# Attention in blocks of 64 for two heads at a time, with row maxima and inverse sums spread through memory, in an attention and mixture-of-experts layer

## The chip, the cores and the metric

The kernel runs on one core of one Trainium2 chip. A core has five engines that run side by side and wait for each other through semaphores: PE (TensorE, matrix products), DVE (VectorE), ACT (ScalarE), POOL (GpSimd) and SP (SyncE, which here only issues transfers). [...] The metric is the time of one execution on the device in microseconds (us), as the median of several runs.

## The reference, cut to what matters

The input x has 8 batches of 512 tokens with 256 features. One normalised copy feeds two branches, and both are added to x.

```python
xn = layernorm(x)                       # 8 x 512 x 256
# attention: 16 heads of 16 features, each query sees keys within 64 positions
q, k, v = split(xn @ Wqkv + bqkv)
scores = q @ k.T * 16 ** -0.5           # per head, 512 x 512
scores = where(abs(i - j) <= 64, scores, finfo.min)
attn = softmax(scores)                  # over keys
a = (attn @ v) @ Wout + bout
# experts: 8 experts, 256 -> 1024 -> 256, the best 2 of each token
f = sum over top 2 of gate * (relu(xn @ w1[e] + b1[e]) @ w2[e] + b2[e])
out = x + a + f
```

All of the matrix products below are in 32-bit floats. One such product appears in the profile as two matmul records.

## The kernel before

**Stages.** The first part (the loop over `UNITS` and `route`) normalises, transposes xn to features by tokens (`xnT`), computes router scores, picks two experts for each token and works out for each of up to 71 expert tiles of 128 slots which tokens it takes. From there on a single loop over `ROUNDS` = 69 rounds of two steps interleaves attention with the expert tiles. Engine order is written out by hand: every engine executes its instructions in the order of the program text, and so does SP with its transfers.

**Expert tiles.** `expert_pieces` gives a list of pieces with a cost: `first_layer(i, 0)` with the transposes of the next tile (9), `second_layer(i - 1)` (16), `first_layer(i, 1)` (8). After the attention work of a step, pieces are popped until the cost done so far reaches the step's share. `first_layer` makes 16 products `h`, and ACT applies bias and ReLU (L808); `turn` transposes gathered tokens (`px`) and DVE copies them (L792); `second_layer` makes 8 products `y` with 256 columns, DVE scales them (L823) and POOL issues a scatter that adds them to the output in memory (L824). `load_1` and `load_2` have SP fetch 1 MB of weights each into buffers that the tile before the last must have left. POOL also issues the gathers of tokens and gates (L715, L725).

**Attention.** The 16 heads of a batch are eight strips of 32 features, a strip holding two heads, `j` = 0 and 1. A *pair* `p` is half a batch: four strips (`a` = 0 to 3, 32 partitions each); there are `PAIRS` = 16. For each pair:

- `dense` (two pairs ahead) makes q and k of the pair. Both exist twice, once for each head of a strip, with the other head's 16 rows zeroed (`at`, `qat`). One row of the zeroed half, `ROW[j]`, is put to use: k holds 1 there, and q will hold minus the row maximum there.
- `maxima(p, n)`, n = 0 to 7, called from `search` one step after another: a block of 128 queries against the 192 or 256 keys of its band (`sc`, four products, 32 rows deep, in two row groups of PE), and then DVE takes with a mask the maximum of each query (L955), negated, into `nms`.
- `put_maxima`: PE transposes `nms` (`nt`), DVE adds it into the free row of q (L977). So the next product gives scores with the maximum already subtracted.
- `weigh(p, n)`: a block of 128 keys against 192 or 256 queries (`st`, four products), ACT takes the exponential from PSUM (L999), POOL zeroes what is outside the band with four selects (L1009, L1014).
- `values(p, n)`: the weights times v (`av`, four products that write 32 partitions each). It runs two units at a time in the first step of the next round. v (`vA`, made by `vals`) has a column of ones per head, so that row `DH * (1 - j)` of the result is the sum of the weights. ACT copies `av` to SBUF (L1045), once for each of the two heads.
- The sums go to memory (`put_sums`), come back 128 partitions wide (`gather_sums`), are inverted (L1067), go to memory (`put_inverses`) and are spread over the 16 rows of each head (`spread_inverses`, eight transfers into `bc`); `scale` multiplies and adds the two heads (L1087, L1088). The table `divide` says in which step of the next pair each runs. For the last pair `scale_at_once` spreads the sums with a product (`den`) instead.
- `project` multiplies with Wout once per batch (`po`), and POOL issues one transfer that adds the batch to the output (L1119).

In step `m` = 2 * round + part the order is: `weigh` of pair p, `search` of unit m + 1 (which belongs to the next pair), on even steps `values` of the two units of the round before, then `dense`, `vals`, `project`, then one step of `divide`, then expert pieces, then on some steps `put_maxima`. On PE a step is therefore st, sc, (av), others, expert products. `weigh` and `search` of one step use opposite strips (`ah` differs), so their products lie in different row groups of PE.

**Buffers that matter.** `st` has one PSUM buffer (`ps_t`), `sc` two (`ps_c`), `av` one (`ps_a`); h, px, y, qk, v, po and nt share three (`ps_m`). The weights `p` have three SBUF buffers.

Of the kernel before, what the change touches and what calls it, by code (L numbers as in the profile page):

```python
# [22 lines left out]
def kernel(  # L23
# [24 lines left out]

    A, G = 4, 4
# [20 lines left out]
    qk_pool = ctx.enter_context(tc.tile_pool(name="qk_pool", bufs=3))  # L70
    o_pool = ctx.enter_context(tc.tile_pool(name="o_pool", bufs=4))
# [64 lines left out]
    raw = p_pool.tile([P, KC, 2 * D], F32, tag="p", name="raw")  # L136
# [46 lines left out]
    for k in range(KC):  # L183
# [21 lines left out]
    mask = const.tile([P, 2 * P], F32, tag="mask", name="mask")  # L205
    nc.gpsimd.memset(mask, 0.0)
    nc.gpsimd.affine_select(
        out=mask, in_=mask, pattern=[[1, 2 * P]], compare_op=ALU.is_ge, fill=NEG,
        base=0, channel_multiplier=-1,
    )  # L210
    nc.gpsimd.affine_select(
        out=mask, in_=mask, pattern=[[-1, 2 * P]], compare_op=ALU.is_ge, fill=NEG,
        base=2 * HALF, channel_multiplier=1,
    )
# [3 lines left out]
    vA, nms = [], []  # L218
    bc = wk1.tile([P, 2, N], F32, tag="bc", name="bc")

    def clear():

        for i in range(2):
            t = wk1.tile([P, NT, NH // 2, 2, 32], F32, tag=f"vA{i}", name=f"vA{i}")
            nc.gpsimd.memset(t.rearrange("p t h j c -> p (t h j c)"), 0.0)
            nc.gpsimd.memset(t[:, :, :, 0, DH : DH + 1], 1.0)
            nc.gpsimd.memset(t[:, :, :, 1, 0:1], 1.0)
            vA.append(t)

        for n in range(2):  # L230
            t = wk1.tile([P, NT, A, 32], F32, tag=f"nm{n}", name=f"nm{n}")
            nc.gpsimd.memset(t.rearrange("p t a r -> p (t a r)"), 0.0)
            nms.append(t)

        nc.gpsimd.memset(bc.rearrange("p j q -> p (j q)"), 0.0)


    ROW = [DH, 0]
# [4 lines left out]
    hot = const.tile([P, 2], F32, tag="hot", name="hot")  # L243
    bqk = const.tile([P, 3, 2], F32, tag="bqk", name="bqk")

    kb_ = const.tile([P, 2, 2], F32, tag="kb", name="kb")
    qb_ = const.tile([P, 2, 2], F32, tag="qb", name="qb")

    def places():
        nc.vector.tensor_scalar(place_i, place_i, 31, None, ALU.bitwise_and)  # L250
        nc.vector.tensor_copy(place, place_i)
        for j, op in enumerate((ALU.is_lt, ALU.is_ge)):
            nc.vector.tensor_scalar(at[:, j : j + 1], place, float(DH), None, op)
            nc.vector.tensor_scalar(hot[:, j : j + 1], place, float(ROW[j]), None, ALU.is_equal)
        nc.vector.tensor_scalar(qat, at, QSCALE, None, ALU.mult)


    choice = const.tile([P, 2, P], F32, tag="choice", name="choice")

    def choices():  # L260
        nc.vector.memset(choice.rearrange("p j m -> p (j m)"), 0.0)
        for j in range(2):
            for a in range(A):
                nc.vector.tensor_copy(
                    choice[32 * a : 32 * a + 32, j, 32 * a : 32 * a + 32],
                    hot[32 * a : 32 * a + 32, j : j + 1].to_broadcast([32, 32]),
                )

    def qk_bias():
        bps = ps_m.tile([P, 512], F32, tag="m", name="bps")  # L270
        transpose(bps[:, 0:6], braw.rearrange("q a r -> q (a r)"), ident[:6, :6])
        nc.scalar.copy(bqk.rearrange("p s i -> p (s i)"), bps[:, 0:6])
        full = [P, 2, 2]
        for to, s, by in ((kb_, 1, at), (qb_, 0, qat)):
            nc.vector.tensor_mul(
                to, bqk[:, s].unsqueeze(2).to_broadcast(full), by.unsqueeze(1).to_broadcast(full)
            )
        nc.vector.tensor_add(kb_, kb_, hot.unsqueeze(1).to_broadcast(full))
# [164 lines left out]
    sel = p_pool.tile([P, 2, TOPK, NA, E], F32, tag="p", name="sel")  # L443
    sel = sel[:, 0]
# [349 lines left out]
    def first_layer(i: int, part: int):  # L794
# [11 lines left out]
        for n in range(HC // 2):  # L806
            c = part * HC // 2 + n
            nc.scalar.activation(  # L808
                s["hT"][:, c, :], ph[:, n, :], AF.Relu, bias=s["tb"][:, c : c + 1]
            )  # L810
# [65 lines left out]
    def reach(t: int):  # L876


        lo, hi = max(0, t * P - HALF), min(N, (t + 1) * P + HALF)
        return lo, hi, lo - (t * P - HALF)  # L880
# [3 lines left out]
    def dense(p: int, s: int, by_act: bool = False, steps=range(KC + 1)):  # L884

        b, i = p // 2, p % 2
        if s == 0 and 0 in steps:
            qk[p] = tuple(
                qk_pool.tile([P, 2, N], F32, tag=n, name=f"{n}_{p}") for n in ("q", "k")
            )  # L890
# [10 lines left out]
        if KC not in steps:  # L901
            return
        for j in range(2):
            to = qk[p][s][:, j, :]
            if s == 1:
                nc.scalar.activation(
                    to, pm, AF.Identity, bias=kb_[:, i, j : j + 1], scale=at[:, j : j + 1]
                )
            elif by_act:
                nc.scalar.activation(  # L910
                    to, pm, AF.Identity, bias=qb_[:, i, j : j + 1], scale=qat[:, j : j + 1]
                )
            else:
                nc.vector.tensor_scalar(
                    to, pm, bqk[:, 0, i : i + 1], qat[:, j : j + 1], ALU.add, ALU.mult
                )

    def vals(b: int, t: int):
        pm = ps_m.tile([P, 512], F32, tag="m", name=f"v_{b}_{t}")
        for k in range(KC):  # L920
            matmul(
                pm[:, 0:D], xnT[b][:, k, ts(t, P)], wv[:, k, :],
                start=(k == 0), stop=(k == KC - 1),
            )

        to = vA[b % 2][:, t].rearrange("p h j c -> p h (j c)").rearrange(
            "p h (u d) -> p h u d", d=DH
        )[:, :, 0:4:3, :]
        nc.scalar.copy(to, pm[:, 0:D].rearrange("p (h j d) -> p h j d", j=2, d=DH))

    first = [(h, j, ah) for h in range(2) for j in range(2) for ah in range(2)]
    second = [(j, h, ah) for j in range(2) for h in range(2) for ah in range(2)]

    def maxima(p: int, n: int):

        half, j, ah = first[n]
        q, k = qk[p]
        sc = []
        for c in range(2):
            sc.append(ps_c.tile([P, 2, 2 * P], F32, tag="c", name=f"sc_{p}_{n}_{c}"))  # L940
        for i in range(2):
            qb = 2 * half + i
            lo, hi, off = reach(qb)
            for c in range(2):
                r = 32 * (2 * ah + c)
                matmul(
                    sc[c][:, i, 0 : hi - lo], q[r : r + 32, j, ts(qb, P)],
                    k[r : r + 32, j, lo:hi], start=True, stop=True,
                )
        for c in range(2):  # L950
            for i in range(2):
                qb = 2 * half + i
                lo, hi, off = reach(qb)
                junk = wk.tile([P, 2 * P], BF16, tag="junk", name=f"jk_{p}_{n}_{c}_{i}")
                nc.vector.tensor_tensor_reduce(  # L955
                    out=junk[:, 0 : hi - lo],
                    in0=sc[c][:, i, 0 : hi - lo],
# [5 lines left out]
                    accum_out=nms[p % 2][:, qb, 2 * ah + c, ROW[j] : ROW[j] + 1],  # L963
                )

    def put_maxima(p: int, half: int):

        pm = ps_m.tile([P, 2 * P], F32, tag="m", name=f"nt_{p}_{half}")
        for i in range(2):
            transpose(  # L970
                pm[:, ts(i, P)],
                nms[p % 2][:, 2 * half + i].rearrange("p a r -> p (a r)"), ident,
            )
        for j in range(2):
            to = qk[p][0][:, j, ts(half, 2 * P)]

            nc.vector.scalar_tensor_tensor(  # L977
                to, pm, at[:, 1 - j : 2 - j], to, ALU.mult, ALU.add
            )
# [3 lines left out]
    def weigh(p: int, n: int):  # L983

        j, half, ah = second[n]
        q, k = qk[p]
        st = ps_t.tile([P, 2, 2, 2 * P], F32, tag="t", name=f"st_{p}_{n}")
        for i in range(2):
            kb = 2 * half + i
            lo, hi, off = reach(kb)  # L990
            for c in range(2):
                r = 32 * (2 * ah + c)
                matmul(
                    st[:, c, i, off : off + hi - lo], k[r : r + 32, j, ts(kb, P)],
                    q[r : r + 32, j, lo:hi], start=True, stop=True,
                )
        w = weights[p, n] = p_pool.tile([P, 2, 2, 2 * P], F32, tag="p", name=f"p_{p}_{n}")
        cut = slice(HALF, 4 * P) if half == 0 else slice(0, 4 * P - HALF)
        nc.scalar.activation(  # L999
            w.rearrange("k c i q -> k c (i q)")[:, :, cut],  # L1000
            st.rearrange("k c i q -> k c (i q)")[:, :, cut],
            AF.Exp,
        )

        for i in range(2):
            lo, hi, off = reach(2 * half + i)
            end = off + hi - lo
            one = w[:, :, i, off:P]
            nc.gpsimd.affine_select(  # L1009
                out=one, in_=one, pattern=[[0, 2], [1, P - off]], compare_op=ALU.is_ge,  # L1010
                fill=0.0, base=off, channel_multiplier=-1,
            )
            two = w[:, :, i, P:end]
            nc.gpsimd.affine_select(  # L1014
                out=two, in_=two, pattern=[[0, 2], [-1, end - P]], compare_op=ALU.is_ge,
                fill=0.0, base=0, channel_multiplier=1,
# [4 lines left out]
    def values(p: int, n: int):  # L1021

        j, half, ah = second[n]
        b, pair = p // 2, p % 2
        if half == 0 and ah == 0:
            av[p, j] = ps_a.tile([P, N], F32, tag="av", name=f"av_{p}_{j}")
        w = weights.pop((p, n))

        for i in range(2):
            kb = 2 * half + i  # L1030
            lo, hi, off = reach(kb)
            for c in range(2):
                a = 2 * ah + c
                matmul(
                    av[p, j][32 * a : 32 * a + 32, lo:hi],
                    vA[b % 2][:, kb, 2 * a + pair, j, :],
# [289 lines left out]
```

## Time and profile before

Three runs took 916.38 us in the median (915.89 to 919.32). The profile is of one execution that took 917.28 us, with a span of 915.2 us; 2.1 us lie around the span. The granted PE clock was 0.987 of full speed over the span.

| What | us | of what |
|---|---|---|
| span of the profiled execution | 915.2 | its time 917.28 |
| ACT bias and ReLU of `hT` | 157.4 | 552 of 0.368 us |
| DVE masked maximum of `sc` | 198.3 | 256 of 0.421 us (256 wide), 256 of 0.354 us (192 wide) |
| ACT exponential | 117.5 | 128 of 0.918 us (896 wide) |
| POOL selects | 285.4 | 384 of 128 x 256, 128 of 128 x 128 |
| DVE add of the maxima into q | 27.8 | 64 of 0.476 us (128 x 256) |
| DVE multiply and add of the division | 29.7 | 15 of 1.257 us, 15 of 0.719 us |
| ACT copy of `av` | 18.7 | 32 of 0.586 us |
| q1, SP's transfers | 57.9% of 16 engines' span | 172.07 MB |
| q0, POOL's transfers | 13.3% of 16 engines' span | 22.33 MB |

Busy time is the sum over an engine's instructions with overlaps counted once. Records of matmuls overlap, so the durations of single ones do not add up to what PE needs for them; the distance from the start of one group to the start of the next does.

### The profile page before, as it was taken

The page shows a single profiled execution, that of the slowest core. Times are in us where ns is not written, and L with a number is a line of the kernel's source. Part 1 is how long each engine was busy: PE and PEld are TensorE (multiplying, and loading weights), DVE is VectorE, ACT ScalarE, POOL GpSimd, SP SyncE. Part 2 cuts the span into 40 slices and gives each one's busy share as a digit, 9 for nine tenths or more (in the row PEclk, how much of TensorE's full clock was granted, in tenths as well). Part 3 has the DMA queues.
Part 4 walks back from the last instruction along what each step waited for, and adds up shares of the span by engine and source line. Part 5 has one row for each costly group of instructions (what it writes and reads, how often), then busy time and mean ns, then how long its engine had stood idle before and what let it go on. Part 6 is the DMA issues. An engine that isn't in the chain of part 4 may idle for free.

```text
span 915.2 us, 20492 instructions
## 1 busy us (share of the span) xinstructions
PE 878.4 (96%) x7264; PEld 704.5 (77%) x7264; DVE 389.5 (43%) x1523; ACT 390.6 (43%) x923; POOL 457.7 (50%) x770
## 2 busy tenths in 40 slices
PE   5878999999999999999999999999999999999896
PEld 2457888788877788887887878777887878888685
DVE  6775533444344434343435343535343434331140
ACT  6652334444543454434443445344534444443231
POOL 4014345555554555464655565555545644664522
PEclk9997999999999999999999999999999999999899
DMA  9954887776675867577767677878777756987763
GB/s 292 315 171 136 242 271 220 222 231 222 199 241 179 215 206 233 172 209 218 221 197 202 200 221 231 211 222 261 219 195 219 235 174 216 250 254 226 195 193 41
DMA packets 154199, 196.26 MB, mean 214 GB/s; under 512 B 26456, under 2 KB 131928, under 8 KB 154096
## 3 DMA queue, kind: packets, MB, share of 16 engines
q1 hardware_dynamic: 133698, 172.07, 57.9%
q0 software_dynamic: 19680, 22.33, 13.3%
q8 instruction: 58, 0.95, 0.4%
q10 hardware_dynamic: 718, 0.54, 0.2%
q14 instruction: 45, 0.37, 0.1%
HBM read 172.71 MB, written 22.18 MB: 213 GB/s over the span
## 4 chain that ended last, share of the span: by engine, by line
PE 91%; DVE 3%; DMA 3%; issue 1%; ACT 1%; POOL 1%; POOLq 0%; DVEq 0%; ACTq 0%
PE h L92 28%; PE y L92 26%; PE st L92 10%; PE av L92 7%; PE qk L92 6%; PE sc L92 4%; PE po L92 4%; PE v L92 3%; PE px L95 2%; DMA x<-in_L_attn_x_dram 1%; DMA out_dram<-yo,dest 1%; PE nt L95 1%; DMA xs<-xd,tok 1%; ACT xn L371 1%; PE xt L95 0%
## 5 line engine op out<-in xcount | busy, mean ns | idle before, releaser
L92 PEld LDWEIGHTS h<-xT,w 128*128 128x128 f32 x2208 | 262.8, 194 | 22.0 <-issue 16.9
L808 ACT ACTIVATE hT<-h,b 128x128 f32<-128x128 f32 x552 | 157.4, 368 | 279.3 <-PE h L92 229.7
L92 PE MATMUL h<-xT,w 128*128 128x128 f32 x2208 | 271.8, 280 | 0.0
L92 PE MATMUL y<-w,hT 128*128 128x256 f32 x1104 | 252.7, 382 | 0.0
L92 PEld LDWEIGHTS y<-w,hT 128*128 128x128 f32 x1104 | 206.0, 190 | 38.7 <-issue 10.4
L824 POOL DMA_INDIRECT out_dram<-yo,dest x69 | 112.1, 1625 | 232.0 <-DVE yo L823 185.5
L955 DVE CUSTOM_DVE_ANT_0 jk<-sc,mask 128x256 bf16<-128x256 f32 (+1 forms) x512 | 170.1, 387 | 117.5 <-PE sc L92 114.2
L999 ACT ACTIVATE p<-st 128x896 f32<-128x896 f32 x128 | 117.5, 918 | 189.9 <-PE sc L92 157.2
L1009 POOL TENSOR_SCALAR_AFFINE_SELECT p<-p 128x256 f32<-128x256 f32 (+1 forms) x256 | 137.3, 563 | 116.2 <-ACT p L999 110.2
L1014 POOL TENSOR_SCALAR_AFFINE_SELECT p<-p 128x256 f32<-128x256 f32 (+1 forms) x256 | 141.2, 582 | 0.0
L92 PE MATMUL sc<-k,q 32*128 32x192 f32 (+1 forms) x1024 | 132.1, 375 | 0.0
L92 PE MATMUL st<-q,k 32*128 32x192 f32 (+1 forms) x1024 | 131.3, 374 | 0.0
L823 DVE SCALAR_TENSOR_TENSOR yo<-y,g,b2g 128x256 f32<-128x256 f32 x69 | 33.4, 484 | 179.7 <-issue 100.0
L92 PEld LDWEIGHTS st<-q,k 32*128 32x128 f32 x1024 | 83.6, 184 | 27.5 <-issue 23.2
L792 DVE COPY xT<-px 128x256 f32<-128x256 f32 x69 | 29.3, 424 | 152.7 <-PE px L95 102.1
L92 PEld LDWEIGHTS sc<-k,q 32*128 32x128 f32 x1024 | 84.1, 185 | 2.2 <-issue 1.8
L715 POOL DMA_INDIRECT xs<-xd,tok x69 | 70.6, 1023 | 24.2 <-issue 10.5
L725 POOL DMA_INDIRECT g<-gd,gate x69 | 65.8, 954 | 21.0 <-issue 20.7
L92 PE MATMUL av<-p,vA 128*32 128x192 f32 (+1 forms) x1024 | 64.7, 360 | 4.3 <-POOL p L1014 4.3
L92 PE MATMUL qk<-xnT,wqk 128*128 128x512 f32 x128 | 62.8, 615 | 0.0
L92 PEld LDWEIGHTS av<-p,vA 128*32 128x32 f32 x1024 | 29.6, 109 | 28.1 <-issue 15.8
L955 DVE DVE_READ_ACCUMULATOR2_ANT nm<- 128x1 f32 x512 | 42.5, 83 | 0.0
(181 smaller groups left out, 584.8 us busy)
## 6 DMA issues: line engine op xcount, KB each, us to landing
w<-in_L_ffn_w_dram SPq DMA_DIRECT2D x120, 1024.0 KB
w<-in_L_ffn_w_dram SPq DMA_DIRECT2D x36, 512.0 KB
b<-in_L_ffn_b_dram SPq DMA_DIRECT2D x69, 128.0 KB
x<-in_L_attn_x_dram SPq DMA_DIRECT2D x8, 512.0 KB
xd<-xn SPq DMA_DIRECT2D x8, 512.0 KB
out_dram<-x SPq DMA_DIRECT2D x8, 512.0 KB
out_dram<-sum POOLq DMA_DIRECT2D x8, 512.0 KB
bc<-d SPq DMA_DIRECT2D x120, 32.0 KB
```

Source lines behind the costliest of these rows:

```text
L92: return pe(nc.tensor.matmul(*args, **kwargs))
L95: return pe(nc.tensor.transpose(*args))
L715: nc.gpsimd.indirect_dma_start(out=tx, out_offset=None, in_=xd, in_offset=bass.IndirectOffsetOnAxis(ap=tok[:, i : i + 1], axis=0),)
L725: nc.gpsimd.indirect_dma_start(out=tg, out_offset=None, in_=gd, in_offset=bass.IndirectOffsetOnAxis(ap=gate[:, i : i + 1], axis=0),)
L792: nc.vector.tensor_copy(s["xT"], px)
L808: nc.scalar.activation(s["hT"][:, c, :], ph[:, n, :], AF.Relu, bias=s["tb"][:, c : c + 1])
L823: nc.vector.scalar_tensor_tensor(yo, py[:, 0:D], s["tg"], b2g, ALU.mult, ALU.add)
L824: nc.gpsimd.indirect_dma_start(out=by_token, out_offset=bass.IndirectOffsetOnAxis(ap=dest[:, i : i + 1], axis=0), in_=yo, in_offset=None, ...
L955: nc.vector.tensor_tensor_reduce(out=junk[:, 0 : hi - lo], in0=sc[c][:, i, 0 : hi - lo], in1=mask[:, off : off + hi - lo], scale=-1.0, sca ...
L999: nc.scalar.activation(w.rearrange("k c i q -> k c (i q)")[:, :, cut], st.rearrange("k c i q -> k c (i q)")[:, :, cut], AF.Exp,)
L1009: nc.gpsimd.affine_select(out=one, in_=one, pattern=[[0, 2], [1, P - off]], compare_op=ALU.is_ge, fill=0.0, base=off, channel_multiplier=-1,)
L1014: nc.gpsimd.affine_select(out=two, in_=two, pattern=[[0, 2], [-1, end - P]], compare_op=ALU.is_ge, fill=0.0, base=0, channel_multiplier=1,)
```

## The change

Blocks are now of `BK` = 64 queries or keys, and one product does both heads of a strip. What is held twice, with the other head zeroed, is the 64-wide block that PE keeps (2 x 64 columns); what streams past is the plain strip. `reach` gives 192 columns (128 at the two ends) instead of 256 and 192. The number of products stays: 512 each of sc, st and av.

```diff
     def reach(t: int):
-        lo, hi = max(0, t * P - HALF), min(N, (t + 1) * P + HALF)
-        return lo, hi, lo - (t * P - HALF)
+        lo, hi = max(0, (t - 1) * BK), min(N, (t + 2) * BK)
+        return lo, hi, lo - (t - 1) * BK
```

`dense` makes q doubled and k plain (k: one ACT operation instead of two); for `weigh` the other way round is needed, and `other_way` makes it: DVE adds the two halves of q, ACT makes k doubled with two operations.

`vals` makes v with the two heads on different halves of the partitions: eight products of 128 columns that write 64 partitions each, instead of two of 256 columns; ACT copies one half, DVE the other.

```diff
+        for n in range(2):
+            for k in range(KC):
+                for j in range(2):
+                    matmul(
+                        pm[ts(j, BK), ts(n, P)], xnT[b][:, k, ts(2 * t + n, BK)],
+                        wv[:, k, :].rearrange("p (h j d) -> p h j d", j=2, d=DH)[:, :, j, :],
+                        start=(k == 0), stop=(k == KC - 1), skip_group_check=True,
+                    )
```

`maxima` keeps the negated masked scores (`less`, 32-bit); a new function `add_up` has ACT take their exponential and sum it, four operations per unit. `invert` has DVE invert the sums of half a pair. The column of ones in v and the copies of `av` go.

```diff
+                    nc.scalar.activation(
+                        one, one, AF.Exp, bias=both[:, 0], scale=-1.0, accum_out=both[:, 1]
+                    )
```

`put_maxima` makes one transpose of 32 rows for half a pair (maxima and inverse sums), DVE copies it, SP writes it to memory with two transfers. `spread_maxima` reads the maxima back over 64 partitions for each head: two transfers of 64 x 4 KB per half pair, into a new tile of `o_pool`. `spread_inverses` still has eight transfers per pair into `bc`, which is now one row set for both heads. `put_sums`, `gather_sums`, `put_inverses`, `scale`, `scale_at_once`, `choices` go.

In `weigh`, DVE adds the spread maxima to the scores from PSUM, two or three operations, and ACT takes the exponential in place in SBUF; the four selects now have 64 partitions with 256 or 128 elements.

```diff
+        for i in range(2):
...
+                    nc.vector.tensor_add(
+                        w[:, :, i, o], st[:, :, i, o],
+                        spread[p, half][:, ts(ah, 2), a - half * H : z - half * H],
+                    )
+        flat = w.rearrange("k c i q -> k c (i q)")[:, :, cut]
+        nc.scalar.activation(flat, flat, AF.Exp)
```

`values` ends with one DVE multiplication of `av` by `bc` into the output of the batch:

```diff
-            nc.scalar.copy(outs[p][:, j, :], av.pop((p, j)))
+            nc.vector.tensor_mul(outs[b][:, pair, :], av.pop(p), bc)
```

`first_layer` gives the ReLU of its second half (`part` 1) to DVE instead of ACT, four operations of 128 x 128 per tile.

The order: `search` now runs three units ahead instead of one, with three units before the first round; `dense(2, 0)` moves from there into the first pair. A new function places the steps of the maxima and sums, called in every step before the expert pieces:

```diff
+    def between(m: int):
+        for p in range(PAIRS):
+            for half in range(2):
+                step = m - 8 * p - 4 * half
+                if step == 1:
+                    invert(p, half)
+                if step == 2:
+                    put_maxima(p, half)
+                if step == 4:
+                    spread_maxima(p, half)
+            step = m - 8 * p
+            if 5 <= step < 8:
+                other_way(p, step - 5)
+            if step == 12:
+                spread_inverses(p)
```

`weigh(p, 0)` is in step 8p + 8. `project` of a batch moves to the rounds 2 and 3 of the even pair that follows it (before: of the odd pair after that; for the last but one batch, rounds 0 and 1 of the last pair). `qk_pool` has two buffers per tag instead of three, `o_pool` six instead of four.

## The prediction

> **What bounds the kernel now.** I read the busy table and the slices first, then the chain that ended last, then PE's timeline in a steady stretch, and last where PE stood still.
>
> ```profile
> PE 878.4 (96%) x7264; PEld 704.5 (77%) x7264; DVE 389.5 (43%) x1523; ACT 390.6 (43%) x923; POOL 457.7 (50%) x770
> PE   5878999999999999999999999999999999999896
> by line: PE h L92 28.2%; PE y L92 25.9%; PE st L92 10.2%; PE av L92 6.5%; PE qk L92 5.6%; PE sc L92 4.1%; PE po L92 3.5%; PE v L92 2.6%; PE px L95 1.7%; issue 1.3%; DMA x<-in_L_attn_x_dram 0.8%; DMA out_dram<-yo,dest 0.8%; PE nt L95 0.8%; D
> ```
>
> PE is full from slice 5 to slice 37, and the chain runs over PE products nearly throughout. So an edit counts by what it does to PE's stream, and other engines count only where PE comes to wait for them. The shares of the chain are PE time without overlap: st and sc together 14.3% of 915.2 = 131 us, av 59.5, v 23.8, nt 7.3.
>
> What a block costs, from PE's timeline (start, duration, group):
>
> ```profile
> 399.62 0.98 PE L92 MATMUL av<-p,vA 128*32 128x256 f32 x16
> 400.53 1.98 PE L92 MATMUL qk<-xnT,wqk 128*128 128x512 f32 x4
> ...
> 404.44 0.43 PE L92 MATMUL st<-q,k 32*128 32x192 f32 x2
> 404.47 0.43 PE L92 MATMUL sc<-k,q 32*128 32x192 f32 x2
> 404.71 0.33 PE L92 MATMUL st<-q,k 32*128 32x192 f32 x2
> 404.74 0.33 PE L92 MATMUL sc<-k,q 32*128 32x192 f32 x2
> 404.87 0.38 PE L92 MATMUL st<-q,k 32*128 32x256 f32 x2
> 404.90 0.38 PE L92 MATMUL sc<-k,q 32*128 32x256 f32 x2
> 405.09 0.38 PE L92 MATMUL st<-q,k 32*128 32x256 f32 x2
> 405.12 0.38 PE L92 MATMUL sc<-k,q 32*128 32x256 f32 x2
> 405.43 3.72 PE L92 MATMUL y<-w,hT 128*128 128x256 f32 x16
> ...
> 417.97 1.03 PE L92 MATMUL v<-wv,xnT 128*128 128x256 f32 x4
> 418.84 3.40 PE L92 MATMUL y<-w,hT 128*128 128x256 f32 x15
> ```
>
> st and sc start within 0.03 us of each other: four row groups work at once. Four records of 192 columns take 0.16 us (404.71 to 404.87), four of 256 take 0.22 (404.87 to 405.09): time goes with columns, 0.84 to 0.86 ns per column over four groups. A block of 16 records takes 0.99 us, of which 2 x 0.16 + 2 x 0.22 = 0.76 is columns and 0.23 start and end.
>
> **The change, PE first.** *st and sc.* The number of products stays, the columns fall from a mean of 224 to 176 (384 of 192, 128 of 128). A block goes to 4 x 0.16 = 0.64 of columns, or 0.54 where the units are at an end of the sequence (0.11 for 128 columns, by the slope); mean 0.59, so 0.17 less. Before, 119 steps have st and sc paired and 9 of each stand alone; with the search three units ahead it is 117 and 11 of each, two blocks more. An unpaired block of eight records took 0.96 (844.27 to 845.23). After: 117 x 0.82 + 22 x 0.79 = 113, 18 less than 131; from the mean block of the chain ((131 - 18 x 0.96) / 119 = 0.956) it is 22. I take -20.
>
> *av.* A group of 16 records takes 0.91 (399.62 to 400.53), of which 4 x 224 x 0.87 ns = 0.78 is columns in each of four column groups; with 176 it is 0.61. 64 x 0.17 = -11.
>
> *nt, den.* 32 transposes instead of 64: half of 7.3, -3.7. The two den products in the chain, -1.7.
>
> *v.* Four records of 256 columns take 0.87 (417.97 to 418.84). Now 16 of 128, writing 64 partitions each, alternating between two column halves. If the halves overlap: 16 x 128 x 0.87 / 2 = 0.89, plus 0.1. If not: 16 at the 0.117 us of h (16 in 1.88) = 1.88. The nearest row for narrow outputs:
>
> ```profile
> 30.76 0.65 PE L92 MATMUL lg<-xnT,rw 128*32 128x128 f32 x16
> 31.33 0.33 PE L95 MATMUL lt<-ident,early 128*128 128x128 f32 x1
> ```
>
> 16 records of 128 columns over four column groups in 0.57: they do overlap, and at 36 ns each they are quicker than anything the narrower st and sc ask for. So +0.1 x 24 = +2; the other end is +1.0 x 24 = +24.
>
> [...]
>
> Sum on PE: -20 - 11 - 3.7 - 1.7 + 2 = **-34 us**.
>
> **A stop that goes.** The one long hole in the loop, near its end:
>
> ```profile
> 853.47 1.64 POOL L824 DMA_INDIRECT out_dram<-yo,dest  x1 [9.23 <-issue]
> 856.89 0.52 PE L92 MATMUL av<-p,vA 128*32 128x192 f32 x4 [1.14 <-POOL p L1014]
> 858.05 0.63 PE L92 MATMUL av<-p,vA 128*32 128x256 f32 x4 [0.64 <-POOL p L1014]
> 861.18 1.77 PE L92 MATMUL av<-p,vA 128*32 128x192 f32 x8 [2.50 <-POOL p L1014]
> ```
>
> The scatter waits behind the transfer that adds a batch to the output (issued at 842.80, in memory only by 853), the selects behind the scatter, av behind the selects: 4.3 us of idle, and then h takes 5.82 instead of 3.84 at a lower clock; with the slow av about 7. It comes from `project` of batch 6 in rounds 0 and 1 of the last pair. After, that lies at the end of pair 14, where the same queue (303.33 sum, 310.04 scatter) cost PE nothing, as two steps lay between. Between 0 and -7: I take **-5**.
>
> **What is added elsewhere.** *DVE:* 256 adds of maxima, 384 wide (between 0.423 of L1117 at 256 and 0.719 of L1088 at 512: 0.57) or 256 (0.42), and 64 of 128 (0.29): 128 x 0.57 + 128 x 0.42 + 64 x 0.29 = 146. ReLU 276 x 0.33 (0.29 of a 128-wide operation, 0.37 of ACT's) = 91. The maxima: 384 x 0.354 + 128 x 0.29 instead of 198: -25. Gone: L977, L1087, L1088, the inversions and the rest of the division, -73. Small ones (v, the final product, q, nt, inverses) +53. 389 + 146 + 91 - 25 - 73 + 53 = 581, 66% of 885. *ACT:* add_up is 512 x 0.42 (0.37 at 128, 0.51 at 256) = 215; hT -79, copies of av -19, exponential -11, k +14: 391 + 120 = 511, 58%. What reading out an accumulated sum costs ACT shows in no row: DVE's read is 0.083, a whole ACT operation 0.37, so 512 x 0.08 to 0.37 = 40 to 190 more, up to 79%; I take the low end, as it is the same kind of read. *POOL:* as many selects of as many elements. *Transfers:* 64 of 256 KB = 16.8 MB; q1 needs 57.9% of 915.2 us for 172.07 MB, 3.08 us per MB, so 52 us; (57.9 + 13.3)% of 915.2 = 652 + 52 is 80% of 885. None is the bound; they are covered by PE as long as each answer comes before PE asks.
>
> *The answer with the least room* is the odd unit of a round: st, DVE add (0.98, or 1.27 split), ACT 0.83, four selects at 0.36 apart (1.44), then av after the next st and sc. From the step's start that is 0.82 + 1.1 + 0.83 + 1.44 + 0.3 for handovers = 4.5. PE asks after 0.82 + 3.65 (a step with one y) + 0.82 = 5.3 in the shortest steps and 6.1 + 0.8 in the mean: 0.8 to 2.4 in hand, where before the same was 1.9 or more, and PE's only idle time on p is the hole above. Behind a late add stand the maxima, xT, yo and now half of the ReLUs; PE reaches those one piece later. Lower bound 0; upper, 64 x 0.4 = 25. I take **+6**.
>
> *The head:* each v now puts 0.42 us on DVE, and eight of them lie where DVE feeds `inv` (57 to 61 us, DVE without gaps); one k operation of ACT less each. 0 to 8 x 0.42 = 3.4; I take **+3**. The three searches lie in the 4.9 us that PE waits for the first gather.
>
> **Sum.** 915.2 - 34 - 5 + 6 + 3 = 885, with 2.1 around the span 887; the profiled run is 0.9 above the median, so **886**.
>
> **The rivals.** *Narrow blocks save nothing* (PE bound by something per product): for it, 0.23 of a block is not columns; against it, the 36 ns of lg. Then -31 goes: 917. *v serial:* +22, 908; for it, no row has outputs of 64 partitions; against it lg. *The maxima come late:* `spread_maxima` of the second half is issued in step 8p + 8 and DVE needs it in 8p + 10, some 13 us later.
>
> ```profile
> SPq L1081 <- DMA d<-rs: 49.1, 8, 8.8
> ```
>
> SP waited up to 8.8 us for a 16 KB transfer, one step old, that queued behind weights; two more of 256 KB make some 10 to 11. For 3 us late in 8 of 16 pairs: 910; against it, the 2 us left. *The slower one: av waits in every round.* Place: the odd unit's chain above. Price: 64 times the excess. To lose the 30 gained it needs 0.5 us of mean excess, that is, engines about 2.5 us late in the mean step. For it: three engines at 58 to 80% in one chain, with add_up ahead of the next exponential on ACT, and a clock that falls when PE stops (5.82 for 3.84). Against it: in the mean step ACT is done with add_up 5 us after the start and has until 8. At 0.8 us: 880 + 51 = 931.
>
> **How the numbers follow.** Forecast 0.66, v serial 0.07, late maxima 0.10, nothing saved 0.05, slower 0.12. Low end: -38 on PE (-22 for st and sc, v free), -7, no waits, no head: 870 and 1.2, so 871. High end: v serial and 5 more of waits, or late maxima: 913; above lie about 0.18. About 0.5% (4.6 us) is what a measurement tells from no change. Faster: 0.64 + 0.07 + 0.04 = 0.75; same 0.08; slower 0.17.
>
> **What would show it.** Blocks of st and sc at 0.8 us and av at 0.75; v near 1.0, not 1.9; PE without idle time before av, st and h, and no hole near the end; ACT near 510, DVE near 580. I am wrong if PE idles on POOL's p or DVE's p in most rounds, or if DVE's add waits for a transfer.

## The result and the profile after

The changed kernel takes 1151.83 us in the median of four runs (1149.26 to 1157.41), the kernel before 917.7 (915.89 to 919.32): a ratio of 1.256, 95% interval 1.2505 to 1.2615. The forecast was 886 with a range of 871 to 913. It was wrong, and in sign.

The page of the changed kernel (profiled execution 1152.21 us, span 1150.4, granted PE clock 0.903), with the lines that answer to those of before: busy times, PE's slices and its granted clock, the chain by engine and by line.

```profile
PE 945.7 (82%) x7612; PEld 743.4 (65%) x7612; DVE 530.5 (46%) x2122; ACT 502.3 (44%) x1653; POOL 463.5 (40%) x765
PE   5769987687978878879997987788797979679796
PEclk9969988897989989889988998888898989788899
PE 42%; DMA 29%; issue 13%; POOL 8%; DVE 4%; ACT 3%; SPq 0%; POOLq 0%; DVEq 0%; ACTq 0%
DMA out_dram<-yo,dest 17%; PE y L94 13%; PE h L94 11%; DMA g<-gd,gate 7%; PE av L94 4%; PE qk L94 4%; POOL p L1077 3%; PE st L94 2%; DMA out_dram<-sum 2%; PE v L94 2%; POOL p L1072 2%; PE po L94 2%; PE sc L94 2%; POOL xs L693 2%; POOL out_d
```

PE had nines in nearly every slice; now it has holes in most of them. No engine took its place: DVE is at 46% and ACT at 44%. What stands in the chain where PE stood is the landing of two transfers, the scatter of the experts' output (17%) and the gather of the gates (7%). Neither belongs to attention. The view of waits says who waits for them (engine, line, for whom: us in total, times, longest us):

```profile
POOL p L1072 <- DMA out_dram<-yo,dest: 221.5, 56, 6.8
PEld av L94 <- POOL p L1077: 176.9, 53, 9.8
PE av L94 <- POOL p L1077: 158.7, 44, 9.5
POOL p L1072 <- DMA g<-gd,gate: 74.7, 39, 5.8
```

POOL stands 296 us ahead of a select on `p` (L1072), and PE stands ahead of `av` for the select behind it. (PE and PEld are the matmuls and the weight loads of the same products, so these two are not added.) Before, PE waited 4.3 us for the selects. The timeline shows which select it is (start, duration, and in brackets the idle time before and what ended it):

```profile
537.77 1.63 POOL L807 DMA_INDIRECT out_dram<-yo,dest  x1 [0.99 <-PE st L94]
539.46 0.41 POOL L1072 TENSOR_SCALAR_AFFINE_SELECT p<-p 64x256 f32<-64x256 f32 x1
539.84 0.42 POOL L1077 TENSOR_SCALAR_AFFINE_SELECT p<-p 64x256 f32<-64x256 f32 x1
544.01 0.42 POOL L1072 TENSOR_SCALAR_AFFINE_SELECT p<-p 64x256 f32<-64x256 f32 x1 [3.76 <-DMA out_dram<-yo,dest]
544.39 0.42 POOL L1077 TENSOR_SCALAR_AFFINE_SELECT p<-p 64x256 f32<-64x256 f32 x1
```

POOL issues the scatter, does two selects (partitions 0 to 63) at once, and then stands 3.76 us ahead of the third, the first on partitions 64 to 127, until the scatter has landed. The selects cost 0.4 us each, as forecast; the wait is what was not. It is in the program: its list of instructions shows, for one unit, a wait of the third select for the semaphores of the transfers that POOL issued (`DMASW`):

```
304 L1072 TensorScalarAffineSelect p_6_4828<-p_6_4828 64x4x64 [waits PE_49,Activation_49]
305 L1077 TensorScalarAffineSelect p_6_4828<-p_6_4828 64x2x64
306 L1072 TensorScalarAffineSelect p_6_4828<-p_6_4828 64x4x64 [waits DMASW7_49,DMASW6_49,DMASW5_49]
307 L1077 TensorScalarAffineSelect p_6_4828<-p_6_4828 64x2x64
```

110 of the 512 selects have such a wait, each on partitions 64 to 127; of the kernel before, none has one.

What a hole (idle time of PE between two products) costs is more than its length. Here is one of 7.55 us; a round without a hole, from the same trace, stands below it:

```profile
502.38 0.74 PE L94 MATMUL av<-p,vA 128*32 128x192 f32 x8
510.66 1.28 PE L94 MATMUL av<-p,vA 128*32 128x192 f32 x8 [7.55 <-POOL p L1077]
...
537.17 0.87 PE L94 MATMUL av<-p,vA 128*32 128x192 f32 x16
```

PE in stretches of 4 us around the hole (the columns are the stretch and its length, then busy time and records of each engine, then the granted clock, the transfers' share and GB/s):

```profile
core 0: us, PE busy (x) PEld busy (x) DVE busy (x) ACT busy (x) POOL busy (x), PEclk, DMA share, GB/s
506.00:510.00 4.00, 0.00 (x0) 0.00 (x0) 0.00 (x0) 0.00 (x0) 0.09 (x1) 0.69 0.72 185
510.00:514.00 4.00, 3.34 (x11) 1.66 (x12) 0.69 (x1) 0.00 (x0) 2.92 (x5) 0.50 0.25 25
514.00:518.00 4.00, 4.00 (x30) 3.37 (x30) 2.65 (x6) 0.00 (x0) 2.54 (x4) 0.96 0.17 35
518.00:522.00 4.00, 4.00 (x35) 3.35 (x34) 2.38 (x13) 2.10 (x6) 0.26 (x2) 1.00 0.84 278
```

PE comes back at half its clock (0.50 in 510 to 514) and has it again some 4 us later (0.96 in 514 to 518, 1.00 in 518 to 522). The length of a hole alone does not say whether this happens. In the same trace a hole of 1.68 us that ends at 1087.74 is followed by 0.50 in 1088 to 1091, and one of 3.18 us that ends at 714.14 by 1.00 all the way to 722; what decides it, no run shows.

To split the loss, I took from PE's timeline the time from the start of each group of products to the start of the next, less the idle time that the trace names ahead of the next (us; four kernels, the last two from the experiments below; the idle time includes some 8.7 us ahead of the first product, and 8.2 to 8.7 us after the last one are in neither):

| | before | after | with multiplications | best version |
|---|---|---|---|---|
| st and sc | 135.1 | 121.5 | 122.4 | 120.3 |
| av | 60.3 | 95.5 | 53.0 | 51.4 |
| v | 30.6 | 36.3 | 34.1 | 33.5 |
| nt | 10.0 | 4.9 | 4.0 | 3.8 |
| h, y | 502.4 | 530.4 | 506.9 | 504.9 |
| qk | 58.1 | 68.3 | 61.6 | 59.4 |
| all products | 878.9 | 946.9 | 867.5 | 857.6 |
| idle ahead of products | 27.7 | 194.9 | 48.1 | 31.0 |
| granted clock | 0.987 | 0.903 | 0.971 | 0.984 |
| span | 915.2 | 1150.4 | 923.8 | 896.8 |

Of the 235.2 us that the span grew, 167.2 are idle time and 68.0 are products. The clock is not all of these 68.0. With each product's time multiplied by the clock granted at its moment, the products come to 870.6 us before, 872.8 after, 846.3 with the multiplications and 846.7 in the best version. So the lower clock costs 74.1 us after and 8.3 before, 65.8 more; the change's own products save 24; and 26 remain, all of them in av (77.8 us in this measure, 51.3 in the best version). They come from the second unit of a round being late: at full clock, av takes 1.41 to 1.62 us when it falls into two parts with a hole between, not counting the hole, and 0.69 to 0.86 in one piece.

### The profile page after: what moved, and what is told of

It reads as the page before. It is cut to its first block, busy times and chain, and to the rows that moved or that the text cites. A ratio compares the mean times of both kernels' runs of the same rounds, so it can differ in the third digit from the quotient of the medians.

```text
span 1150.4 us, 23064 instructions
## 1 busy us (share of the span) xinstructions
PE 945.7 (82%) x7612; PEld 743.4 (65%) x7612; DVE 530.5 (46%) x2122; ACT 502.3 (44%) x1653; POOL 463.5 (40%) x765
## 4 chain that ended last, share of the span: by engine, by line
PE 42%; DMA 29%; issue 13%; POOL 8%; DVE 4%; ACT 3%; SPq 0%; POOLq 0%; DVEq 0%; ACTq 0%
DMA out_dram<-yo,dest 17%; PE y L94 13%; PE h L94 11%; DMA g<-gd,gate 7%; PE av L94 4%; PE qk L94 4%; POOL p L1077 3%; PE st L94 2%; DMA out_dram<-sum 2%; PE v L94 2%; POOL p L1072 2%; PE po L94 2%; PE sc L94 2%; POOL xs L693 2%; POOL out_dram L807 1%
## 5 line engine op out<-in xcount | busy, mean ns | idle before, releaser
L1067 ACT ACTIVATE p<-p 128x640 f32<-128x640 f32 (+1 forms) x128 | 101.1, 790 | 401.2 <-DVE p L1061 383.8
L1072 POOL TENSOR_SCALAR_AFFINE_SELECT p<-p 64x256 f32<-64x256 f32 (+1 forms) x256 | 101.8, 398 | 386.2 <-DMA out_dram<-yo,dest 221.5
L94 PE MATMUL av<-p,vA 128*32 128x192 f32 (+1 forms) x1024 | 99.6, 357 | 159.0 <-POOL p L1077 158.7
L988 ACT ACTIVATE less<-less,nm 128x192 f32<-128x192 f32 (+1 forms) x512 | 218.2, 427 | 16.2 <-DVE nm L965 15.0
L1061 DVE TENSOR_TENSOR p<-st,mx 128x384 f32<-128x384 f32 (+2 forms) x320 | 126.3, 444 | 46.5 <-PE st L94 28.2
L787 ACT ACTIVATE hT<-h,b 128x128 f32<-128x128 f32 x276 | 78.2, 364 | 157.2 <-PE h L94 129.3
L965 DVE CUSTOM_DVE_ANT_0 less<-sc,mask 128x192 f32<-128x192 f32 (+1 forms) x512 | 142.9, 335 | 5.9 <-PE sc L94 4.6
L94 PE MATMUL st<-qf,kh 32*128 32x192 f32 (+1 forms) x1024 | 111.1, 334 | 5.4 <-ACT kh L916 5.2
L791 DVE TENSOR_SCALAR hT<-h,b 128x128 f32<-128x128 f32 x276 | 77.3, 343 | 63.5 <-PE h L94 59.4
L1077 POOL TENSOR_SCALAR_AFFINE_SELECT p<-p 64x256 f32<-64x256 f32 (+1 forms) x256 | 103.5, 404 | 0.0
L94 PEld LDWEIGHTS st<-qf,kh 32*128 32x128 f32 x1024 | 76.7, 184 | 34.8 <-issue 16.6
L988 ACT ACTIVATION_READ_ACCUMULATOR less<-less,nm 128x1 f32 x512 | 95.9, 187 | 0.0
L693 POOL DMA_INDIRECT xs<-xd,tok x69 | 68.4, 991 | 33.5 <-POOL p L1077 13.7
```

Source lines behind the costliest of these rows:

```text
L94: return pe(nc.tensor.matmul(*args, **kwargs))
L693: nc.gpsimd.indirect_dma_start(out=tx, out_offset=None, in_=xd, in_offset=bass.IndirectOffsetOnAxis(ap=tok[:, i : i + 1], axis=0),)
L787: nc.scalar.activation(s["hT"][:, c, :], ph[:, n, :], AF.Relu, bias=s["tb"][:, c : c + 1])
L791: nc.vector.tensor_scalar(s["hT"][:, c, :], ph[:, n, :], s["tb"][:, c : c + 1], 0.0, ALU.add, ALU.max)
L965: nc.vector.tensor_tensor_reduce(out=less[:, c, i, off : off + hi - lo], in0=sc[c][:, i, off : off + hi - lo], in1=mask[:, off : off + hi ...
L988: nc.scalar.activation(one, one, AF.Exp, bias=both[:, 0], scale=-1.0, accum_out=both[:, 1])
```

## The experiments

**Are the upper partitions the cause?** Three kernels. The first keeps the result and does without selects on part of the partitions: a table of ones and zeros, made once, and two multiplications per unit on all 128 partitions.

```diff
-        for j in range(2):
-            front = w[ts(j, BK), :, 1 if t == 0 else 0 :, 0:BK]
-            nc.gpsimd.affine_select(
...
+        n = 1 if t == 0 else 2
+        front = w[:, :, 2 - n : 2, 0:BK]
+        full = [P, 2, n, BK]
+        nc.gpsimd.tensor_mul(
+            front, front, inband[:, 0].unsqueeze(1).unsqueeze(1).to_broadcast(full)
+        )
...
```

> The changed kernel with the four selects of a unit, each on one half of the partitions, replaced by two POOL multiplications by a table of ones and zeros, each on all 128 partitions; the result is the same. In the changed kernel POOL stood 296 us ahead of the select on the upper partitions, by the profile for the scatter (221.5) and the gather of gates (74.7), and PE 336 us ahead of av for that select (158.7 + 176.9, matmuls and weight loads of the same products). Theory A: that wait, for transfers that have nothing to do with the select, is the whole of the loss, and the program without it has no such wait. Then: 870 to 910 us, no idle time of POOL on the multiplication named for a transfer, PE's clock back near 1.0. Rival B: the chain st, add, exponential, mask, av is too long by itself, since ACT and DVE carry more (ACT 502 us, DVE 530), and PE would only wait for other names: 1060 to 1160 us. Rival C: half of each, 960 to 1040.

Measured: 925.32 us (923.71 to 925.65), ratio to before 1.0083 (1.0051 to 1.0115). 226 of the 234 us are gone. POOL's wait ahead of the mask is now for the exponential, as it should be:

```profile
POOL p L1082 <- ACT p L1076: 150.6, 88, 6.3
```

Theory A had the cause, but not the time: 925 lies 15 above its range. Something of the change costs time besides the wait. The other two kernels leave out half of the selects each, so that the band is cut out for half of the keys only:

```diff
-        for j in range(2):
+        for j in range(1):        # lower only
+        for j in range(1, 2):     # upper only
```

> The changed kernel with the two selects on partitions 64 to 127 left out, so the band is not cut out for half of the keys; the two selects on partitions 0 to 63 stay. Theory A (only an instruction on the upper partitions waits for POOL's transfers): 870 to 910 us, and POOL's idle time ahead of the selects named for ACT, not for a transfer. Rival B (the chain is too long, or ACT and DVE too full): the chain is shorter by two selects, 0.8 us, so 1060 to 1130. Rival C (the number of selects decides): about the same as the run with the upper ones only.

> The changed kernel with the two selects on partitions 0 to 63 left out, so the band is not cut out for the other half of the keys; the two selects on partitions 64 to 127 stay. As many instructions of as many elements are gone as in the run with the lower ones only, so the two differ in nothing but the partitions. Theory A: the wait for the scatter and the gathers stays, 1080 to 1150 us, with some 56 waits for the scatter of up to 7 us. Rival B: within 2% of the run with the lower ones only. Rival C: likewise.

Measured: 924.42 us with the lower ones, 1148.49 with the upper ones (one run each). The waits of POOL ahead of its selects, first with the lower ones:

```profile
POOL p L1072 <- ACT p L1067: 167.3, 93, 5.1
```

then with the upper ones:

```profile
POOL p L1072 <- DMA out_dram<-yo,dest: 232.4, 46, 9.0
POOL p L1072 <- DMA g<-gd,gate: 101.3, 35, 7.4
```

The two programs differ in nothing but the partitions, and by 224 us. So neither the number of selects nor the load of DVE and ACT makes the loss (rivals B and C fall); the upper half alone does. Without the two selects on the lower half it is no smaller (1148.49 against 1151.83). The programs say the same: 110 selects wait for POOL's transfers with the upper ones, none with the lower ones.

**Does the old kernel get it too?** Each of its selects cut into two, once by partitions and once by columns:

```diff
+            for j in range(2):
+                one = w[ts(j, 64), :, i, off:P]
...
+            for c in range(2):
+                one = w[:, c, i, off:P]
...
```

> The kernel before, with nothing of the change in it, but each of its selects (128 partitions) cut into two, one on partitions 0 to 63 and one on partitions 64 to 127; the result is the same. Eight selects of 0.40 us a unit (64 partitions, 256 elements, as in the changed kernel's rows) are 3.2 us where four made 2.4. Theory A (a select on the upper partitions alone waits for the transfers that POOL issued): the old kernel gets the loss without any of the change's other parts, 1080 to 1220 us, with long waits of POOL for the scatter and of PE for the select. Rival B (the changed kernel's longer chain is what makes such a wait cost anything; before, PE had its answers 1.9 us or more early): 915 to 960 us.

> The kernel before with each of its selects cut into two by its columns, both on all 128 partitions; the result is the same. As many selects as in the run cut by partitions, of 128 elements each (0.48 us by the rows of before), so POOL's work is larger still: 8 x 0.48 = 3.9 us a unit. Theory A: no wait for a transfer, 915 to 950 us. Rival B (more and shorter selects cost what they cost, on whichever partitions): as the run cut by partitions or slower.

Measured: 1240.43 us by partitions, 921.47 by columns (one run each; before 916.7). By partitions:

```profile
POOL p L1010 <- DMA out_dram<-yo,dest: 207.1, 54, 7.0
PE av L92 <- POOL p L1015: 191.8, 105, 12.2
```

By columns POOL has as many instructions, and waits for ACT:

```profile
POOL p L1010 <- ACT p L999: 83.7, 57, 3.5
```

109 selects wait for POOL's transfers in the program cut by partitions, none in the one cut by columns. The loss needs nothing of the change except the selects' partitions, and it comes out above the range that theory A gave (1080 to 1220).

**What else costs time?** From here on the edits are on top of the multiplications. The rows that decide where to look, in that kernel's trace: PE's waits, and DVE in the head, between the choice of experts and the sizes.

```profile
PE inv L94 <- DVE tl L561: 10.1, 3, 6.4
PE st L94 <- ACT kh L925: 5.2, 4, 2.2
PE av L94 <- POOL p L1088: 5.1, 2, 2.8
PE h L94 <- DMA w<-in_L_ffn_w_dram: 4.7, 3, 3.4
```

```profile
45.16 0.69 DVE L487 TENSOR_TENSOR_SCAN upto<-goon,took 128x256 bf16<-128x256 bf16 x1
51.85 0.43 DVE L947 COPY vA<-v 64x256 f32<-64x256 f32 x1 [6.00 <-ACT vA L945]
52.72 0.43 DVE L947 COPY vA<-v 64x256 f32<-64x256 f32 x1 [0.45 <-ACT vA L945]
53.16 0.17 DVE L509 TENSOR_SCALAR size_i<-ranks 128x8 int32<-128x8 f32 x1
```

`size_i` reads products that PE began at 45.90 and 46.34, but two copies of v stand ahead of it in DVE's queue, and v comes behind four products of q and k on PE. Before, `size_i` ran at 43.79, 1.83 us after `upto`; here it is 8.0 us after. The edit gives these copies to ACT:

```diff
-            if j == 0:
+            if j == 0 or b < 2:
                 nc.scalar.copy(to, of)
```

> The changed kernel with the multiplications in the selects' place (925.3 us) and one edit more: for batches 0 and 1, whose v is made ahead of the loop, ACT copies the lower and the upper half of v, where DVE copied the upper one. In the trace with the multiplications DVE stands 6.0 us in the routing's chain (at 45.9 to 51.9) ahead of a copy of v, which waits for PE and ACT, and the first y comes 11.4 us later than before. Theory D (an in-order wait in DVE's queue delays the head): 6 to 9 us less, 916 to 919 us, and the first yo of the experts at 90 to 93 us instead of 99. Rival (the head is late for the 0.43 us that each copy takes DVE, 8 x 0.43 = 3.4, or for the three searches): 922 to 925.

Measured: 913.22 us (910.71 to 915.23), ratio 0.9946 (0.9929 to 0.9962), and the first `yo` (the scaled output of the first expert tile) at 89.11 instead of 99.05 (87.69 before). Theory D holds, with more than it asked for: 12 us less, not 6 to 9. Next the keys:

```diff
-            if 5 <= step < 8:
-                other_way(p, step - 5)
+            if 2 <= step < 5:
+                other_way(p, step - 2)
```

> As the run with the head's copies on ACT, and the keys and queries laid out the other way are made three steps earlier (steps 2 to 4 of a pair instead of 5 to 7). In the trace with the multiplications st waited four times for ACT's key copies, 5.2 us, and h once for ACT's sums, 1.5 us, each followed by a lower clock. Theory E (what is left of the loss in the loop is single late answers, each with a stretch of lower clock behind it): 5 to 10 us less than the run with the head's edit alone, 906 to 914 us, and no wait of st for ACT. Rival F (ACT is too full, so a key copy made earlier only puts another ACT operation in the late place): within 2 us of it.

Measured: 908.12 us (906.85 to 908.84), ratio 0.9900 (0.9873 to 0.9926). PE no longer waits for ACT's keys, and the time is 5.1 us lower, so theory E holds as to the late answers. Its stretches of lower clock do not show as it says: of the four waits for keys, one (2.15 us, ended at 597.5) is followed by a lower clock (0.74 in 596 to 600, 0.84 in 600 to 604), the others and the one for the sums by 1.00. Now weights are its longest wait in the loop, and SP's timeline shows what stood ahead of them:

```profile
PE h L94 <- DMA w<-in_L_ffn_w_dram: 7.5, 4, 3.5
PE av L94 <- POOL p L1088: 6.1, 3, 2.6
```

```profile
143.07 6.76 SPq L1038 DMA_DIRECT2D bc<-d  x8
149.87 1.10 SPq L1027 DMA_DIRECT2D mx<-d  x2
151.81 0.41 SPq L745 DMA_DIRECT2D w<-in_L_ffn_w_dram  x1
```

The edit issues two of the eight transfers of inverse sums in each of four steps (`a` becomes an argument):

```diff
-            if step == 12:
-                spread_inverses(p)
+            if 9 <= step < 13:
+                spread_inverses(p, step - 9)
```

> As the run with the keys made earlier (908.1 us), and the eight transfers that spread a pair's inverse sums are issued two by two in steps 9 to 12 instead of all in step 12. In its trace these eight take SP 6.8 us in a row (143.07 to 149.83), and PE then waits for weights 7.5 us in all, 3.5 of it at 159 in the same round. Theory G (SP's time to issue, not the bytes, makes the weights late): the waits for weights fall below 2 us, and the time by 5 to 12 us, clock included: 896 to 903. Rival H (the transfers' own share, 80% with 16.8 MB of maxima, makes the weights late): the waits stay, 906 to 910.

Measured: 897.52 us (894.99 to 903.01), ratio 0.9804 (0.9758 to 0.9849). In the same place two of these transfers took 0.91 us and the weights went out 5 us earlier, at 146.75; PE's wait for weights fell to 1.0 us, although the bytes are the same. Theory G holds. This version, the best one of the table above, is faster than both kernels. The last of these edits moves the maxima:

```diff
-                if step == 4:
+                if step == 3:
                     spread_maxima(p, half)
```

> As the run with the inverse sums apart, and the transfers that spread the maxima are issued a step earlier (one step after they went to memory instead of two). In the trace with the keys made earlier DVE's add stood for a late maximum (1.23 us at 644, and 3.7 at 380 in the one before it), and PE behind it for the mask (6.1 us in all) and for nt (1.9). Theory: the late maxima go and those waits shrink, 2 to 6 us less than the run with the inverse sums apart. Rival: SP now waits for the maxima to land in memory and holds up weights behind it: 0 to 8 us more.

Measured: 904.23 us (900.95 to 908.87), ratio 0.9871 (0.9828 to 0.9915), so 6.7 us more in the medians, where the ranges of the two kernels' four runs overlap (up to 903.01, from 900.95). The late maxima do go: DVE's wait for them falls from 12.8 us to 0.4. But SP now stands for the maxima to reach memory before it may read them back, as the rival said. The rival's late weights do not show (PE's wait for weights was 1.0 us and is now under 0.2); what grows is PE's wait for masks, from 5.1 us, and why they come later stays open:

```profile
SPq L1027 <- DMA d<-nt: 29.1, 17, 5.6
```

```profile
PE av L94 <- POOL p L1088: 12.1, 7, 3.6
```

**Would the small edits have shown beside the wait?** The changed kernel with its selects and all three good edits:

> The changed kernel with its four selects as they were, and with the three small edits (the head's copies on ACT, the keys earlier, the inverse sums apart), which took 27.8 us off the kernel with the multiplications (925.3 to 897.5). Theory I (in the loop the selects' wait is the last to end in most rounds and hides the small ones; only the head, 11 to 12 us, lies outside it): 1136 to 1143 us. Rival (the costs add up): 1122 to 1127. Rival (whatever comes early only waits longer, the head too): 1147 to 1155.

Measured: 1150.95 us (one run), no gain that can be told from the 1149.26 to 1157.41 of the changed kernel. The third expectation holds, the head included: its first `yo` came 10.4 us earlier (90.18 instead of 100.60), the 40th 2.8 earlier, the 69th 1.2. PE's wait for the selects grew to 177.4 us:

```profile
PE av L94 <- POOL p L1077: 177.4, 48, 11.2
```

## Why the prediction was wrong, by its own steps

*"POOL: as many selects of as many elements"* is the step that failed. The count was right (0.40 us each, four per unit) and so was the chain of the odd unit in which they stand. But only what was the same was compared (number and elements), and what had changed, the partitions, was passed over: each of the 110 waits comes from it. The prediction's own sign of being wrong, PE idle on POOL's p in most rounds, is what came: 44 such waits in 64 rounds, 158.7 us. What a moved or re-cut instruction waits for belongs to its price, and the list of instructions of the changed program held it before any run.

*The waits, +6 (0 to 25).* They were 167 us of idle time, and with it 66 of lower clock and 26 of av in two parts. The slower rival had the right place, av waiting for the odd unit's chain, but the wrong mechanism and size: it let engines come late through their load, and priced 0.8 us a round, without the clock. Its reason for was "a clock that falls when PE stops"; that half came (0.903 over the span, 0.987 before). Without the wait on transfers PE stands 5.1 us for the masks, so +6 was fair for what the step had in view.

*The sum on PE, -34.* It is -21.3 in the best version (857.6 against 878.9), at nearly the clock of before, and -23.9 with each product's time multiplied by the granted clock. st and sc gave -14.8 (forecast -20), av -8.9 (-11), nt -6.2 (-3.7), v +2.9 (+2); h, y and qk, which the change does not touch, took 3.8 more. The mechanisms were right, and the sum was half as large again as what came. The rival that narrow blocks save nothing falls, and so does a serial v.

*A stop that goes, -5.* From the 64th to the 69th `yo` it is 51.8 us before and 41.0 with the multiplications: -10.8. The hole lies in that stretch, with the slow clock behind it (0.50 in 861.2 to 866.2); how much of the 10.8 is the hole was not separated.

*The head, +3.* It was 11.4 with the multiplications (first `yo` at 99.05 against 87.69). The step counted what each copy of v takes DVE (0.42 us) and not what it waits for in an in-order queue ahead of the routing (6.00 us). With the copies on ACT 1.4 us remained.

*What the prediction had no term for:* the key copies on ACT and the eight transfers of inverse sums on SP, each late for PE now and then. It listed the transfers' bytes, not SP's time to issue them. Each such hole was 0.2 to 3.5 us; the edits that took them away brought 5 us and, by the ratios 0.9900 and 0.9804 of two comparisons, about 9.

*The other engines.* DVE 530 (forecast 581), ACT 502 (511), transfers 78% with the multiplications (80). The 511 leaves out the reading of the accumulated sums, for which the prediction took the low end of 40 to 190; with it the forecast is 551. ACT's reading lasts 0.187 us, but its next instruction starts 0.093 us after the reading does (522.03 and 522.12 in one place), so 512 of them add some 48 us: near the low end, and not the bound. Late maxima, a rival with 23 us, made DVE wait 10.8 us in five places with the multiplications; most of that stayed off PE, which waited 5.1 us for masks in two places.

So with the one wait gone and three smaller late answers out of the way, the change is worth 18 us (897.52 against 915.64), where 30 were forecast.

## What to carry to other kernels

An instruction is not priced by its count and size alone: ask what the built program makes it wait for, and compare that list before and after, above all when its partitions change or when its engine also issues transfers (here 110 waits against none). An operation put into an in-order queue costs what it waits for there, not what it takes (6.00 us against 0.43 for a copy of v). And take the dominant wait away first: edits worth 26 to 28 us without it (by the ratios and by the medians) showed no gain beside it.

## What the runs showed of the hardware and was not expected

A POOL select on partitions 64 to 127 alone is made, in the program as it is built, to wait until transfers that POOL issued have landed; one on partitions 0 to 63 or on all 128 is not (110 waits against 0 among the 256 selects of each of the two half kernels, 1148 against 924 us; 0 among the 512 selects on 128 partitions of the kernel before). Whether the chip needs this wait was not tried: no run leaves it out and keeps such a select.

POOL's multiplication of 128 x 256 by a broadcast table took 0.77 to 0.78 us, two selects of 64 x 256 0.86, one select of 128 x 256 in the kernel before 0.59 to 0.62: on these rows the table is no dearer than the two half selects, and dearer than one whole one.

ACT reads an accumulated sum out with an instruction of its own. It lasts 0.187 us, more than twice DVE's 0.083, and sets ACT's next instruction back by 0.093.

Eight small transfers that spread one row over 16 partitions held SP 6.76 us in a row, two of them 0.91 (0.85 us each against 0.46). With the same bytes to move, PE's wait for weights fell from 7.5 us to 1.0 when they were issued two by two: the weights had been late for the queue that issues them, not for their bytes.

Two units of av in one piece took 0.69 to 0.86 us at full clock, the same products in two pieces 1.41 to 1.62, without the hole between them: here a late second half cost PE 0.55 to 0.93 us beside its wait.
